# A two-layer graph network on one core: where the second softmax of a pair gets its exps, its store and its fetch

## The chip, the cores and the metric

The kernel runs on one core of a Trainium2 chip. The metric is the device time of one execution in microseconds (us). Before the change the median of three executions is 2647.58 us (2642.99 to 2649.26); the profiled execution has a span of 2647.7 us. All times below are of that profile, in us from the start of the span. The engines are TensorE (PE, its weight loads PEld), VectorE (DVE), ScalarE (ACT), GpSimd (POOL) and SyncE (SP), which issues nearly all transfers.

## What is computed

The input is x, 128 batches of 128 nodes by 512 features in float32, and adj, 128 batches of 128 by 128 flags. Layer 0 is masked attention with 8 heads of 64, layer 1 an attention over the same mask whose logits are sums of a node's two scalars. Both add their result to their input and normalise each row.

```python
# layer 0
q, k, v = x @ Wq + bq, x @ Wk + bk, x @ Wv + bv        # 8 heads of 64
logits  = einsum('bqhd,bkhd->bhqk', q, k) / 8
attn    = softmax(where(adj > 0, logits, -1e9), axis=-1)
x = layernorm(x + relu(einsum('bhqk,bkhd->bqhd', attn, v) @ Wo + bo))
# layer 1
Wh = x @ W
e  = leaky((Wh @ a1)[:, :, None] + (Wh @ a2)[:, None, :])
x  = layernorm(x + leaky(softmax(where(adj > 0, e, -9e15), axis=1) @ Wh))
```

## The kernel before

**Products.** All arithmetic is float32. Products with weights are done by Strassen's scheme with seven block products p1 to p7 (`ORDER`). Q, K and V are computed for a *group* of four batches at once (`group_product`, L367), the products of layer 0 with Wo and of layer 1 with W for a *pair* of batches (`pair_product`, L448). Each scheme is cut into seven steps: p1 with the read-out t0, p5, p6 with t2, p2 with c11, p7 with t3 and c22, p4 with c21, p3 with c12. The read-outs t0, t2, t3 are ScalarE copies (`st_t` at L344 or L348 for groups, `pr_t` at L459 for pairs), and p6, p7 and p4 add to the bank that they have just read, so TensorE can't go on with that bank until the copy is done. The results c11 to c12 are VectorE additions (L385, L693, L697, L772) or ScalarE copies. The group's banks are three of their own; all others (`psum`) share five in turn.

**Steps.** The main loop runs t from -3 to 123, one step for each batch; the last four batches follow by a written plan (`PLAN`). Every engine has its own queue, and the order in each is the order of the program (`manual_schedule`): there is no scheduler, and an instruction that waits holds all that follow on its engine. `group(n)` and `pair(n)` emit the next n pieces of the running group and pair products between the other work. In an even step t the pair product is layer 1's for batches t-6 and t-5, in an odd one layer 0's for t-3 and t-2. Each step also carries one batch of layer 1's attention (`Edge`, called `edge`, `fin` and `coming` in its three stages).

**Attention, around which the change is.** It goes by pairs of batches: `first` is the softmax of batch t, `sm` that of t+1, t even.
- `scores` (L520): TensorE forms the logits of both at the start of the even step, four banks.
- `maxima` = `add` (L534, mask onto the logits, VectorE) and `reduce` (L543).
- `exp` (L554) and `divide` (L568): one ScalarE instruction for each head, with `reciprocals` (L564, VectorE) between. An exp is followed by the read of its sum.
- `store` (L575) writes the weights to DRAM, `fetch` (L581) reads them back in four transfers with blocks of 32 moved, and `transpose` (L587, VectorE) turns the blocks: together the transposed weights.
- `attend` (L600): O^T = V^T times the transposed weights, eight products of 64 by 128 each way; `copy` (L614) reads it out with a bias on ScalarE, and `sum` forms the sums for the next product on GpSimd.

In an even step `first` does its exps, divisions, store and fetch, and at its end `sm` does exps 0 to 3 (L1183 to L1187). In the odd step `sm` does exps 4 to 7 among the pieces of layer 0, then its divisions, the last two after the fourth group piece (L1163); `sm.store` and `sm.fetch` stand behind all of that (L1170, L1176), and between the two stands the fetch of the edge's logits (`ez`, L1175). `sm.transpose` is the last VectorE piece before the two `attend` at the end of the odd step (L1193 to L1203). After `attend` come the scores of the next pair.

In the steps 0 to 3 there is not yet work of layer 1, and other branches of the loop give the order (L1030 to L1067).

Of the kernel before, what the change touches and what calls it, by code (L numbers as in the profile page):

```python
# [8 lines left out]
F32 = mybir.dt.float32  # L9
# [15 lines left out]
def kernel(  # L25
# [68 lines left out]
    big = ctx.enter_context(tc.tile_pool(name="big", bufs=2))  # L94
    work = ctx.enter_context(tc.tile_pool(name="work", bufs=1))
# [158 lines left out]
    def load_residual(b):  # L254

        X1[b] = work.tile([P, D], F32, name="x1", bufs=7)
        nc.sync.dma_start(X1[b], x[b])
# [610 lines left out]
    def on(b):  # L868
        return 0 <= b < B
# [14 lines left out]
    none = Nothing()  # L884
# [16 lines left out]
    first = sm = fin = edge = coming = none  # L901
# [77 lines left out]

    chores += right_blocks(places(wk)) + load_wv()  # L980
    END = B - GROUP
    for t in range(-3, END):
        pair_steps = []
        if t % GROUP == 1 and on(t + 3):
            rest = group_steps
            group_steps, v_pieces, fetch_v = products((t + 3) // GROUP)
            group_steps = rest + group_steps
        if t % 2 == 1 and on(t - 3):
            pair_steps = zero[(t - 3) // 2] = LayerZero((t - 3) // 2)
            pair_steps = pair_steps.steps()  # L990
        if t % 2 == 0 and on(t - 6):
            pair_steps = LayerOne((t - 6) // 2).steps()

        def group(n=1):
            for _ in range(min(n, len(group_steps))):
                group_steps.pop(0)()
            for _ in range(min((3 if t == -3 else 2 if t >= 0 else 1) * n, len(chores))):
                chores.pop(0)()

        def w1_chores(n):  # L1000
            for op in [w1_sums.pop(0) for _ in range(n)]:
                op()

        def pair(n=1):
            for _ in range(min(n, len(pair_steps))):
                pair_steps.pop(0)()

        if on(t + 2):
            load_mask(t + 2)
        if t == 0:  # L1010
            load_blocks(Wo, columns(wo), nc.sync, spread_rows=False)
            late_chores = right_blocks(places(wo)) + load_bias()
            w1_loads, w1_sums, w1_blocks = load_w1()
        if t == 1:
            chores += late_chores

        if t % 2 == 0:

            first, sm = (Softmax(t), Softmax(t + 1)) if on(t) else (none, none)
            first.scores()  # L1020
            sm.scores()
        coming.turn_blocks()
        if t % 2 == 1 and on(t - 3):
            zero[(t - 3) // 2].by()
            zero[(t - 3) // 2].bw()
        if later and t > 4:
            later.pop().go_back()
        if t == 5:
            group(2)
        if t < 3 and t % 2 == 0:  # L1030
            first.maxima()
            sm.add(0)
            sm.add(1)
            group(2)
            if on(t - 2):
                load_residual(t - 2)
            if t == 0 and on(GROUP):
                sum_x(1)()
            first.exp(0, 1, 2, 3)
            group()  # L1040
            first.reciprocals(0)
            first.exp(4, 5, 6, 7)
            first.reciprocals(1)
            sm.reduce()
            first.divide(0, 1, 2, 3)
            group()
            first.divide(4, 5, 6, 7)
            mask_float(t + 2)
        elif t < 3:
            group(2)  # L1050
            if on(t - 2):
                load_residual(t - 2)
            sm.exp(4, 5)
            group()
            sm.exp(6, 7)
            sm.reciprocals(0)
            sm.reciprocals(1)
            if t == 1:
                group()
            sm.divide(0, 1, 2, 3)  # L1060
            first.transpose()
            group()
            sm.divide(4, 5, 6, 7)
            if t == 1:
                group()
            if on(t + 2):
                mask_float(t + 2)  # L1067
        elif t == 4:

            layer = later.pop()  # L1070
            first.maxima()
            group()
            layer.apply(0)
            sm.add(0)
            sm.add(1)
            load_residual(2)
            if on(8):
                sum_x(2)()
            first.exp(0, 1)
            group()  # L1080
            first.exp(2, 3, 4, 5)
            sm.reduce()
            group()
            layer.store(1)
            layer.store(0)
            layer.fetch(1)
            layer.fetch(0)
            w1_chores(3)
            first.exp(6, 7)
            group()  # L1090
            first.reciprocals(0)
            first.reciprocals(1)
            first.divide(0, 1, 2, 3, 4, 5, 6, 7)
            mask_float(6)
        else:
            if t % 2 == 0:
                first.maxima()
            group()
            if t % 2 == 0:
                sm.add(0)  # L1100
                sm.add(1)
            if t == 3:
                w1_chores(3)
            if t == 5:
                turn_x1(4)
                x1_sums()
            edge = coming
            edge.add()
            fin.residual()
            if on(t - 2):  # L1110
                load_residual(t - 2)
            edge.maxima()
            fin.stats()
            fin.rstd()
            x1_sums()
            if t % GROUP == 0 and on(t + GROUP):
                sum_x(t // GROUP + 1)()
            pair()
            if t % 2 == 0:
                first.exp(0, 1, 2, 3)  # L1120
            else:
                sm.exp(4, 5)
            edge.exp()
            pair()
            if t % 2 == 0:
                first.exp(4, 5)
                sm.reduce()
            else:
                sm.exp(6, 7)
                first.transpose()  # L1130
            group()
            (first if t % 2 == 0 else sm).reciprocals(0)
            pair()
            if t % 2 == 0:
                first.exp(6)
            else:
                sm.reciprocals(1)
            fin.apply()
            fin.store()
            if t % 2 == 0:  # L1140
                first.exp(7)
            else:
                sm.divide(0, 1)
            edge.divide()
            pair()
            if t % 2 == 0:
                first.reciprocals(1)
                first.divide(0, 1, 2, 3)
            else:
                sm.divide(2, 3, 4, 5)  # L1150
            coming = Edge(t - 6) if on(t - 6) and t + 1 < END else none
            coming.sender()
            coming.store_sender()
            if t in (3, 5):
                w1_chores(2 if t == 3 else 4)
            if t == 5:
                for op in w1_blocks:
                    op()
            group()
            if t % 2 == 0:  # L1160
                first.divide(4, 5)
            else:
                sm.divide(6, 7)  # L1163
            pair()
            if t % 2 == 0:
                first.divide(6, 7)
            if on(t + 2):
                mask_float(t + 2)
            group()
        (first if t % 2 == 0 else sm).store()  # L1170
        if 0 <= t < 3:
            for load in w1_loads[4 * t : 4 * t + 4]:
                load()
        if t >= 6:
            coming.fetch_sender()  # L1175
        (first if t % 2 == 0 else sm).fetch()  # L1176
        for b in x_turns(t):
            transpose_x(b)
        for b in x_turns(t + 1):
            load_x(b)  # L1180
        if on(t + 2):
            mask(t + 2)
        if t % 2 == 0:  # L1183
            sm.exp(0, 1)
        pair(2)
        if t % 2 == 0:
            sm.exp(2, 3)  # L1187
        if t % 2 == 0 and on(t - 6):
            turn_x1(t)
        if t not in (0, 4):  # L1190
            group(21 if t % GROUP == 0 else 1)
        if t % 2 == 1:
            sm.transpose()  # L1193
        fin = edge
        fin.product()
        fin.copy()
        if t % 2 == 1:

            first.attend()
            sm.attend()  # L1200
            first.copy()
            sm.copy()
            sm.sum(0, 1, 2, 3)  # L1203

# [65 lines left out]
    for n in range(4):  # L1272
        jobs[f"s{n}"] = Softmax(END + n, homes[n])
    jobs["al"] = later.pop()
# [112 lines left out]
```

## Time and profile before

| | before |
|---|---|
| median of 3 executions | 2647.58 us |
| span of the profile | 2647.7 us |
| mean granted TensorE clock | 0.955 |
| TensorE without work | 207.7 us (span less busy 2440.0) |
| VectorE, ScalarE, GpSimd busy | 1810.6, 1515.2, 796.9 us |
| transfers | 395.31 MB, 149 GB/s; 48.4% of 16 engines in the main queue |
| four steps in the steady part (t = 7 to 123) | 81.2 us |
| store of 512 KB of weights, issue to landing (median) | 3.1 us |
| fetch of 128 KB of weights, issue to landing (median) | 2.8 us |

How to read it: the busy share of TensorE is an average and its ends are modelled, so the table says where there is time without work but not why. The waits of an engine, with the releaser beside each, say which work came last. The timeline then shows that work in order. The granted clock is a column of its own when the profile is cut into short windows: TensorE that is busy at a lower clock does less.

### The profile page before, as it was taken

The numbers are of one execution on the slowest core, as the hardware profiler recorded it, in microseconds if no ns is written. First come the engines' busy times: TensorE is split into PE (matmuls) and PEld (weight loads), VectorE is DVE, ScalarE is ACT, GpSimd is POOL, SyncE is SP. The second block draws the span as 40 slices with busy tenths as digits, with TensorE's granted clock in tenths as the row PEclk, the third lists the DMA queues.
The fourth block names the chain that finished last, engine by engine and source line by source line (L and its number), as shares of the span: only waits on it lengthen the run. The fifth ranks groups of instructions, "written<-read, shape, count | busy, mean of one in ns | idle before, by whom it ended". The sixth has DMA issues, their size and how long they took to land.

```text
span 2647.7 us, 44071 instructions
## 1 busy us (share of the span) xinstructions
PE 2440.0 (92%) x13362; PEld 2069.0 (78%) x13362; DVE 1810.6 (68%) x3718; ACT 1515.2 (57%) x5459; POOL 796.9 (30%) x1191
## 2 busy tenths in 40 slices
PE   8789999999999999999999999999999999999997
PEld 7678778778787787787877877878778778778775
DVE  5557666766767676667667676766666767766668
ACT  3546556555565565555655655655556555555575
POOL 1222332322323233323223232332222333322325
PEclk9899999999999999999999999999999999999999
DMA  7444454454445445444454444444444544454443
GB/s 203 131 144 147 148 156 146 147 154 146 148 143 157 150 142 155 151 151 148 149 158 151 142 152 150 143 153 149 149 147 142 161 151 148 149 156 149 141 151 117
DMA packets 435564, 395.31 MB, mean 149 GB/s; under 512 B 108280, under 2 KB 339328, under 8 KB 435328
## 3 DMA queue, kind: packets, MB, share of 16 engines
q1 hardware_dynamic: 435008, 392.23, 48.4%
q8 instruction: 107, 1.75, 0.3%
q14 instruction: 129, 1.06, 0.1%
q10 hardware_dynamic: 320, 0.26, 0.0%
HBM read 248.58 MB, written 143.72 MB: 148 GB/s over the span
## 4 chain that ended last, share of the span: by engine, by line
PE 59%; DMA 15%; DVE 10%; ACT 7%; SPq 5%; issue 3%; POOL 1%; DVEq 0%; POOLq 0%; ACTq 0%
PE st_y L367 16%; PE st_w L367 10%; PE p_y L448 10%; PE lg L520 7%; DMA pa_dram<-pa 7%; DMA paz<-pa_dram 6%; PE p_w L448 5%; DVE pa L587 4%; ACT pa L568 4%; PE st_x L367 4%; SPq L581 4%; PE p_oT L600 3%; PE p_x L448 3%; PE p_h L841 2%; DMA xz<-in_x_dram 1%
## 5 line engine op out<-in xcount | busy, mean ns | idle before, releaser
L650 POOL TENSOR_SCALAR ve<-mv 128x1 f32<-128x1 f32 x256 | 70.2, 274 | 1415.5 <-DVE mv L646 1410.0
L554 ACT ACTIVATE pa<-pa,nmax 128x128 f32<-128x128 f32 x1008 | 394.1, 395 | 3.4 <-DVE nmax L543 3.4
L568 ACT ACTIVATE pa<-pa,rs 128x128 f32<-128x128 f32 x1008 | 327.2, 393 | 26.5 <-DVE rs L564 26.2
L600 PE MATMUL p_oT<-pa,v 128*64 128x128 f32 x2016 | 160.2, 309 | 177.3 <-DVE pa L587 176.9
L600 PEld LDWEIGHTS p_oT<-pa,v 128*64 128x64 f32 x2016 | 124.4, 152 | 238.5 <-DVE pa L587 191.8
L534 DVE TENSOR_TENSOR pa<-lg,mf 128x512 f32<-128x512 f32 x252 | 161.7, 683 | 170.2 <-PE lg L520 170.2
L614 ACT ACTIVATE oT<-p_oT,b_cols 128x128 f32<-128x128 f32 x504 | 143.7, 368 | 223.5 <-PE p_oT L600 222.4
L459 ACT COPY pr_t<-p_y 128x257 f32<-128x257 f32 (+1 forms) x375 | 138.1, 368 | 203.3 <-PE p_y L448 201.2
L344 ACT COPY st_t<-st_y 128x512 f32<-128x512 f32 x192 | 110.3, 574 | 192.8 <-PE st_y L367 192.5
L587 DVE STREAM_TRANSPOSE pa<-paz 128x1024 f32<-128x1024 f32 x126 | 156.7, 1244 | 80.3 <-DMA paz<-pa_dram 79.3
L520 PE MATMUL lg<-kT,qT 64*128 64x128 f32 x2048 | 204.9, 377 | 0.0
L520 PEld LDWEIGHTS lg<-kT,qT 64*128 64x128 f32 x2048 | 189.7, 282 | 17.5 <-issue 17.1
L554 ACT ACTIVATION_READ_ACCUMULATOR pa<-pa,nmax 128x1 f32 x1008 | 193.5, 192 | 0.0
L652 POOL TENSOR_TENSOR rstd<-ve,mhalf 128x1 f32<-128x1 f32 x256 | 176.4, 689 | 21.3
L348 ACT ACTIVATE st_t<-st_y,b_cols 128x256 f32<-128x256 f32 x192 | 80.4, 469 | 159.7 <-PE st_y L367 159.6
L543 DVE TENSOR_REDUCE nmax<-pa 128x8 f32<-128x1024 f32 x126 | 151.7, 1204 | 2.3
L276 POOL TENSOR_TENSOR oS<-oT 128x256 f32<-128x256 f32 x63 | 45.7, 725 | 314.0 <-ACT oT L614 314.0
L448 PE MATMUL p_y<-wo,oT 128*128 128x256 f32 x504 | 129.9, 380 | 4.5 <-ACT p_y L469 3.1
L448 PE MATMUL p_y<-wo,oS 128*128 128x256 f32 x504 | 129.5, 379 | 0.5 <-ACT pr_t L459 0.5
L448 PE MATMUL p_y<-w,x1T 128*128 128x257 f32 x496 | 128.3, 381 | 1.8 <-ACT wk L459 1.8
L448 PE MATMUL p_y<-w,x1S 128*128 128x257 f32 x496 | 128.0, 380 | 0.2 <-ACT wk L459 0.2
L367 PE MATMUL st_y<-xT,wk 128*128 128x256 f32 x512 | 126.3, 390 | 0.0
(201 smaller groups left out, 5920.5 us busy)
## 6 DMA issues: line engine op xcount, KB each, us to landing
pa_dram<-pa SPq DMA_DIRECT2D x126, 512.0 KB, 3.1
paz<-pa_dram SPq DMA_DIRECT2D x504, 128.0 KB, 2.8
wv_n<-wv SPq DMA_DIRECT2D x224, 256.0 KB, 2.7
x<-in_x_dram SPq DMA_DIRECT2D x128, 256.0 KB, 2.9
x_dram<-x SPq DMA_DIRECT2D x128, 256.0 KB, 2.1
xz<-x_dram SPq DMA_DIRECT2D x512, 64.0 KB, 2.0
xz<-in_x_dram SPq DMA_DIRECT2D x496, 64.0 KB, 2.3
out_dram<-z SPq DMA_DIRECT2D x120, 256.0 KB, 2.0
```

Of the source, the lines that this page charges most:

```text
L367: nc.tensor.matmul(p[:, m, :], lhs, rhs, start=start and m == 0 and kc == 0, stop=True, skip_group_check=True,)
L448: nc.tensor.matmul(p[:, :width], xs()[n][:, kc, :], w[:, PLACE[n], kc, :], start=start and kc == 0, stop=True, skip_group_check=True,)
L459: nc.scalar.copy(t[:, :width], p[:, :width])
L520: nc.tensor.matmul(self.lg[r][:, c, :], q[rows, c, cols], k[rows, c, cols], start=c == 0, stop=True, skip_group_check=True,)
L534: nc.vector.tensor_add(by_head[:, r * NC : (r + 1) * NC], self.lg[r].rearrange("p c (b k) -> p c b k", b=4), mf.unsqueeze(1).to_broadcast( ...
L543: nc.vector.tensor_reduce(self.nmax, by_head, AX.XY, ALU.max, negate=True)
L554: nc.scalar.activation(self.pa[:, :, h, :], self.pa[:, :, h, :], AF.Exp, bias=self.nmax[:, h : h + 1], accum_out=self.sums[:, h : h + 1],)
L568: nc.scalar.activation(self.pa[:, :, h, :], self.pa[:, :, h, :], AF.Copy, scale=self.rs[:, h : h + 1])
L587: nc.vector.transpose(self.paT.rearrange("p h (a i) -> p a h i", i=32), self.paz.rearrange("p a (h k) -> p a h k", k=32),)
L600: nc.tensor.matmul(self.oT[r * HD : (r + 1) * HD, c, :], v[:, h * HD : (h + 1) * HD], self.paT[:, r * NC + c, :], start=c == 0, stop=True, ...
L614: nc.scalar.activation(OT[pair][:, c, h * P : (h + 1) * P], self.oT[:, c, :], AF.Identity, bias=b_cols[:, 1, c : c + 1],)
L652: nc.gpsimd.tensor_tensor(self.r, ve, mhalf, ALU.pow)
```

## The change

It reorders the second softmax of each pair (`sm`) and moves the first O^T of the kernel.

- Its exps: 0 to 5 at the end of the even step (three before and three after the next-to-last pair piece), 6 and 7 at the start of the odd step, ahead of the odd step's first pieces.
- Its reciprocals in the odd step come right after the edge's residual, ahead of the edge's maxima; its divisions are drawn together to the third pair piece, with `sm.store` right behind them. Before, the store stood at the end of the step.
- Its fetch comes ahead of the fetch of the edge's logits, and its transpose ahead of the last piece of the pair product (p3 with c12 of layer 0, and what follows it on VectorE), which it stood behind.
- The O^T of batches 0 and 1, which ended step 1, is held until the end of step 2, and `sm.transpose` of batch 1 goes into step 2. As their weights live longer, batches 2 and 3 get their weights' tile in buffers of other tags (`x1T` and `v`), through the `homes` argument that `Softmax` has already.

The aim is that the transposed weights of `sm` are there when TensorE reaches its O^T. The core of the diff ("..." where lines are left out):

```diff
+    first_homes = {
+        2: {"pa": lambda shape: work.tile(shape, F32, name="pa", tag="x1T")},
+        3: {"pa": lambda shape: big.tile(shape, F32, name="pa", tag="v", bufs=3)},
+    }
...
+        if t % 2 == 1:
+            sm.exp(6, 7)
         if t == 5:
             group(2)
...
             first.divide(0, 1, 2, 3)
+            if t == 2:
+                held[1].transpose()
...
-            sm.exp(4, 5)
             group()
-            sm.exp(6, 7)
             sm.reciprocals(0)
...
             fin.residual()
             if on(t - 2):
                 load_residual(t - 2)
+            if t % 2 == 1:
+                sm.reciprocals(0)
+                sm.reciprocals(1)
             edge.maxima()
...
             else:
-                sm.divide(2, 3, 4, 5)
+                pair()
+                sm.divide(0, 1)
+                edge.exp()
+                sm.divide(2)
+                pair()
+                sm.divide(3, 4, 5)
+                first.transpose()
+                group()
+                pair()
+                fin.apply()
+                fin.store()
+                sm.divide(6, 7)
+                sm.store()
+                edge.divide()
+                pair()
...
-        (first if t % 2 == 0 else sm).store()
+        if t % 2 == 0:
+            first.store()
+        elif t < 3:
+            sm.store()
...
+        if t % 2 == 1:
+            sm.fetch()
         if t >= 6:
             coming.fetch_sender()
-        (first if t % 2 == 0 else sm).fetch()
+        if t % 2 == 0:
+            first.fetch()
...
         if t % 2 == 0:
-            sm.exp(0, 1)
-        pair(2)
+            sm.exp(0, 1, 2)
+        pair()
+        if t % 2 == 1 and t != 1:
+            sm.transpose()
+        pair()
         if t % 2 == 0:
-            sm.exp(2, 3)
+            sm.exp(3, 4, 5)
...
-        if t % 2 == 1:
-            sm.transpose()
         fin = edge
         fin.product()
         fin.copy()
-        if t % 2 == 1:
-
-            first.attend()
-            sm.attend()
-            first.copy()
-            sm.copy()
-            sm.sum(0, 1, 2, 3)
+        if t == 1:
+            held = first, sm
+        elif t == 2 or t % 2 == 1:
+
+            both = held if t == 2 else (first, sm)
+            for softmax in both:
+                softmax.attend()
+            for softmax in both:
+                softmax.copy()
+            both[1].sum(0, 1, 2, 3)
```

More of the change, by code (lines that the diff above doesn't have):

```diff
@@ L1017 @@
         if t % 2 == 0:
-            first, sm = (Softmax(t), Softmax(t + 1)) if on(t) else (none, none)
+            first, sm = none, none
+            if on(t):
+                first, sm = (Softmax(b, first_homes.get(b)) for b in (t, t + 1))
             first.scores()
@@ L1117 @@
                 sum_x(t // GROUP + 1)()
-            pair()
             if t % 2 == 0:
+                pair()
                 first.exp(0, 1, 2, 3)
[L1121 to L1125, printed above, removed]
+                edge.exp()
+                pair()
                 first.exp(4, 5)
                 sm.reduce()
[L1128 to L1134, printed above, removed]
-                first.exp(6)
[L1136 to L1140, printed above, removed]
-                first.exp(7)
[L1142 to L1146, printed above, removed]
+                group()
+                first.reciprocals(0)
+                pair()
+                first.exp(6)
+                fin.apply()
+                fin.store()
+                first.exp(7)
+                edge.divide()
+                pair()
                 first.reciprocals(1)
@@ L1149 @@
             else:
-                sm.divide(2, 3, 4, 5)
+                pair()
+                sm.divide(0, 1)
+                edge.exp()
+                sm.divide(2)
+                pair()
+                sm.divide(3, 4, 5)
+                first.transpose()
+                group()
+                pair()
+                fin.apply()
+                fin.store()
+                sm.divide(6, 7)
+                sm.store()
+                edge.divide()
+                pair()
             coming = Edge(t - 6) if on(t - 6) and t + 1 < END else none
@@ L1161 @@
                 first.divide(4, 5)
-            else:
-                sm.divide(6, 7)
             pair()
@@ L1183 @@
         if t % 2 == 0:
-            sm.exp(0, 1)
-        pair(2)
+            sm.exp(0, 1, 2)
+        pair()
+        if t % 2 == 1 and t != 1:
+            sm.transpose()
+        pair()
         if t % 2 == 0:
-            sm.exp(2, 3)
+            sm.exp(3, 4, 5)
         if t % 2 == 0 and on(t - 6):
```

## Prediction

> **What bounds the kernel now.** I read the page's first two parts, then the waits of TensorE, then the timeline around the longest of them, then the granted clock in short windows. TensorE is busy 92% of the span and the chain that ended last is mostly its own work:
>
> ```profile
> PE 2440.0 (92%) x13362; PEld 2069.0 (78%) x13362; DVE 1810.6 (68%) x3718; ACT 1515.2 (57%) x5459; POOL 796.9 (30%) x1191
> ...
> PE 59%; DMA 15%; DVE 10%; ACT 7%; SPq 5%; issue 3%; POOL 1%; DVEq 0%; POOLq 0%; ACTq 0%
> ```
>
> One wait makes up nearly all the rest (columns: us in total, times, longest). It comes once in each pair of steps:
>
> ```profile
> PE p_oT L600 <- DVE pa L587: 176.9, 62, 7.1
> PE p_h L841 <- DVE wk L836: 4.3, 4, 2.6
> ```
>
> It is the O^T of the second batch of a pair (`sm.attend`), which waits for the block transpose of its weights, which waits for a store and a fetch through DRAM. The timeline of one pair (start, duration) shows the chain and what follows it:
>
> ```profile
> 1035.88 0.32 SPq L575 DMA_DIRECT2D pa_dram<-pa  x1
> ...
> 1038.84 2.23 SPq L581 DMA_DIRECT2D paz<-pa_dram  x4
> ...
> 1043.86 1.25 DVE L587 STREAM_TRANSPOSE pa<-paz 128x1024 f32<-128x1024 f32 x1 [0.56 <-DMA paz<-pa_dram]
> ...
> 1045.16 1.51 PE L600 MATMUL p_oT<-pa,v 128*64 128x128 f32 x16 [2.83 <-DVE pa L587]
> ...
> 1046.60 3.24 PE L520 MATMUL lg<-kT,qT 64*128 64x128 f32 x32
> ```
>
> The clock granted to TensorE (the number after the five busy times) is full before the gap and falls after it:
>
> ```profile
> 1036.00:1040.00 4.00, 4.00 (x20) 3.54 (x19) 3.78 (x8) 0.32 (x2) 0.00 (x0) 1.00 0.46 152
> 1040.00:1044.00 4.00, 2.33 (x21) 1.28 (x19) 3.31 (x9) 2.56 (x7) 2.25 (x4) 1.00 0.71 197
> 1044.00:1048.00 4.00, 2.84 (x28) 2.51 (x30) 1.73 (x3) 1.14 (x4) 0.08 (x1) 0.71 0.54 172
> ```
>
> So the gap is paid twice: 2.83 us of idleness, and then scores that take 3.24 us. In a pair where the clock happened to stay up, the same scores take 2.06:
>
> ```profile
> 1166.77 1.09 PE L600 MATMUL p_oT<-pa,v 128*64 128x128 f32 x16 [3.25 <-DVE pa L587]
> 1167.80 2.06 PE L520 MATMUL lg<-kT,qT 64*128 64x128 f32 x32
> ```
>
> **What the Trainium skill says.** "TensorE: Matmul & The Clock Gate", Part 1 (the HAM clock gate), describes two clock states, full and half, with a fall after an idle window of about 3.4 us and a return after about as long of work. The trace agrees on the half and on the length (half-clock from 1045.8 to 1049), but gaps of 2.17 us already bring it on in most pairs; gaps of 1.90, 1.66 and 1.42 us elsewhere in this trace left the clock full. "DMA: Bandwidth & Descriptors", Rules for kernel authors, says a DMA that reads what an earlier one wrote must wait for that one's completion; the trace agrees, the fetch starts 2.96 us after the store. "PSUM — Partial Sum Buffer", Engine vs sequencer instructions, says ScalarE and VectorE queues are strictly first in, first out; the trace agrees, the last two divisions of the second batch stand behind a bias copy that waits for TensorE (below).
>
> **What a group of four steps costs.** Call pair A the steps t%4 = 0, 1 and pair B t%4 = 2, 3. From the second O^T of a pair to that of the next, less the wait, A takes 37.1 us at full clock (1166.77 to 1206.09, less 2.18). B takes 37.0 with slow scores (1045.16 to 1085.55, less 3.38); it has one group product fewer (10 against 11, 1.73 us each), so 35.4 at full clock, and a slow clock costs 1.6. Four steps of full-clock work: 72.5. From the second O^T of t=7 (189.23) to that of t=123 (2544.31) are 29 such groups, 81.2 us each: 72.5, about 5.6 of waits (A 2.4, B 3.2) and 3.1 of slow clock.
>
> **The change part by part.** It adds and removes no instruction of compute; TensorE's order is the same after t=2. All effects are waits.
>
> *Exps.* The second batch's exps 4 and 5 go to the end of the even step, 6 and 7 to the start of the odd one. Two exps are 0.77 us (start to start 0.385). At the end of the even step ScalarE is idle 1.06 us before `v<-st_y` and 2.00 before `z<-p_h`: hidden, cost nothing. In the odd step exps 6 and 7 stand ahead of the bias copy, `e_turned` and `pr_t`; `pr_t` comes about 0.15 us later and its reader on TensorE (p6 at 1030.79) keeps over 1 us: nothing.
>
> *Division and store, pair A.* Before, six divisions ran at 1032.12 and the last two only at 1035.17, behind the bias copy of a group product that ended on TensorE at 1034.44. Now all eight are due before it: reciprocals at about 1028, four exps and divisions follow, the last two come after `pr_t` of p6 (readable at 1031.85), so at 32.2 to 32.8. Store at 1032.85 for 1035.88, 3.0 us sooner. In pair B, ScalarE: divisions from 1069.55, `st_t` at 71.75, `pr_t` 72.2, last two 72.5 to 73.1. But the output store stands ahead on the DMA queue and waits for VectorE, which now does the transpose and the kT addition first: about 1073.7. Store at about 1074.05 for 1075.96, 1.9 sooner.
>
> *Fetch and transpose.* Store to landing is 2.90 us in the A sample and 3.97 in B, where a weight load lay just ahead; I take 2.9 and 3.3. Fetch to landing is 4.9 and 4.1. Transpose and semaphore 1.3. A: 1032.85+2.9+4.9+1.3 = 1042.0, while the first batch's O^T ends at 1042.1: no wait left. B: 1074.05+3.3+4.1+1.3 = 1082.75 against 1081.95: 0.8 left (0.3 to 1.8 with landings of 2.9 to 3.97 and the store a little off). Both are below the 1.9 that left the clock full: no slow scores. The fetch of `ez` goes behind that of `paz`: 1.8 us later, and its reader comes after the transpose: nothing.
>
> *The wait that moves.* `sm.transpose` now stands ahead of the last block of LayerZero on VectorE. Behind it queue y, residual, statistics, two `apply`, an addition and `e_turned`: 3.2 to 3.8 us from the end of the transpose (0.39+0.69+0.69+0.18+0.51+0.27+0.51, gaps, and 0.68 in A). The first to wait for these is the bank of the next scores, which y frees: transpose end +0.45, scores at +0.87: nothing. Then the additions of the mask to the scores start at 3.7 us after the second O^T instead of 2.2. In the full-clock sample everything after them on VectorE is without a break until c11 of LayerOne, and its slack is small:
>
> ```profile
> 1179.46 0.40 ACT L798 ACTIVATE e<-mf,wh 128x128 f32<-128x128 bf16 x1 [0.90 <-DVE wh L772]
> ...
> 1180.35 0.35 ACT L459 COPY pr_t<-p_y 128x257 f32<-128x257 f32 x1
> ```
>
> TensorE adds p4 to that bank at 1181.14, 0.44 us after. So 1.5 us later costs TensorE about 1.0 in A's even step. For B, a pair with the additions at +3.8 (1209.91) has `pr_t` at +14.7 where full-clock TensorE is due at +14.4: 0.25. The unknown is how much VectorE slips: 0 to 1.8 us for A and B together.
>
> *Start.* First O^T moved behind t=2's products: the wait of 7.07 us goes, and one slow start. t=2's scores start at 65.3 instead of 75.34. But the eight copies of O^T (2.3 us) and two more exps lie ahead of the LayerZero bias on ScalarE: p_y at about 81.6 instead of 91.90, a new wait of some 2 us. Gain 10; then 3 at t=3 (3.48 before) and 3 for each of the next two pairs: 19. The two `pa` tiles in other buffers add no wait: x1T is first written at t=5, and the v buffers at t=4.
>
> *Sum.* 72.5 + 0 + 0.8 + 1.0 + 0.25 + 0.25 for jitter of the transfers = 74.8 a group; 6.4 us less, times 29 = 186; with the start 205; 2647.6 - 205 = about 2443 us.
>
> **Rivals.** (1) VectorE catches up and nothing new waits: 73.1 a group, 81.2-73.1 = 8.1, times 29 = 235, and 19: 2394. For it: DVE 68% busy. Against it: the unbroken row after the scores. (2) The clock keeps falling, or stalls at p4 and a late fetch eat more: 3 us a group more than forecast, 2530. For it: 2.17 us was enough for the slow clock; a stall and a late store in B could come near it. Against: 1.90 did not. (3) Slower: the store leaves no sooner since ScalarE or the output store ahead of it holds it, while VectorE, which now waits for the fetch with LayerZero's last block behind it, hands its 3.7 us on to the next scores: 1.5 us more a pair for 62 pairs, less 10 for the start: 2647.6 + 83 = 2731. Against it: the last two divisions lose the very wait that held them.
>
> **How the numbers follow.** Forecast 0.62, rival 1 0.14, rival 2 0.2, rival 3 0.04. Time 2443; range 2398 to 2525, from just above rival 1 to nearly rival 2. Faster 0.95, same 0.01, slower 0.04.
>
> **What would show it.** The wait of p_oT on L587 falls from 176.9 to some 30 us; the mean clock rises from 0.955 to 0.98 or more and the scores take 2.06 us in most pairs; the store follows p6's `pr_t` in A; new waits of TensorE for `pr_t` (L459) appear, more in A. Wrong would be: scores still at 3.2 to 3.8, or a wait on VectorE where the scores' bank is freed.

## The result, and the profile after

The changed kernel takes 2459.68 us (median of 4 runs, 2457.11 to 2464.29), against 2645.28 us (4 runs, 2635.23 to 2649.26) for the kernel before in the same comparison. The ratio is 0.9306, 95% interval 0.9275 to 0.9336: about 186 us less. The forecast was 2443.

The page's busy times and the chain of work that ended last, by engine, after the change:

```profile
PE 2355.6 (96%) x13362; PEld 1972.3 (80%) x13362; DVE 1836.2 (75%) x3718; ACT 1517.7 (62%) x5459; POOL 770.5 (31%) x1191
...
PE 45%; DVE 25%; DMA 11%; ACT 9%; SPq 4%; issue 4%; POOL 1%; DVEq 0%; POOLq 0%; ACTq 0%
```

The profiled span fell from 2647.7 to 2457.2 us, and TensorE is busy for 96% of it instead of 92%. Its own busy time fell too, by 84.4 us, with the same 13362 matmuls: the same work ran at a higher clock (mean granted clock 0.997, before 0.955). The chain has moved a step: DMA's share went from 15% to 11%, and VectorE's from 10% to 25%. VectorE comes up again below.

The waits of TensorE after the change (us in total, times, longest):

```profile
PE p_y L448 <- ACT pr_t L459: 36.6, 44, 1.2
PE p_oT L600 <- DVE pa L587: 32.9, 34, 3.1
PE p_h L841 <- DVE wk L836: 5.0, 5, 2.6
```

The wait of O^T for the transpose has gone from 176.9 us to 32.9, and from 62 occurrences to 34. A wait that was not among those shown of before now leads the list: a product of layer 1 (`LayerOne` in the kernel, as `LayerZero` is layer 0) that waits for ScalarE's read-out copy `pr_t`.

The timeline (start, duration) of a pair B, then, after the "...", of the pair A that follows it:

```profile
1061.30 0.34 SPq L865 DMA_DIRECT2D out_dram<-z  x1
1061.74 0.38 SPq L575 DMA_DIRECT2D pa_dram<-pa  x1
...
1064.61 3.16 SPq L581 DMA_DIRECT2D paz<-pa_dram  x4
...
1071.52 1.09 PE L600 MATMUL p_oT<-pa,v 128*64 128x128 f32 x16 [1.66 <-DVE pa L587]
...
1072.54 2.06 PE L520 MATMUL lg<-kT,qT 64*128 64x128 f32 x32
...
1100.63 0.33 SPq L575 DMA_DIRECT2D pa_dram<-pa  x1
...
1103.31 1.75 SPq L581 DMA_DIRECT2D paz<-pa_dram  x4
...
1108.11 1.25 DVE L587 STREAM_TRANSPOSE pa<-paz 128x1024 f32<-128x1024 f32 x1
...
1109.03 1.97 PE L600 MATMUL p_oT<-pa,v 128*64 128x128 f32 x32
1110.92 2.06 PE L520 MATMUL lg<-kT,qT 64*128 64x128 f32 x32
```

In pair A both O^T now run in one go (`x32`, no bracket): the transpose starts with the first matmuls of the output product before them and is done under the first O^T. In pair B a wait of 1.66 us is left, and the scores behind it still take 2.06 us, so the clock stays up. The clock in the three 4 us windows around pair A's O^T (five busy times, then the granted clock, the DMA share and GB/s) says the same:

```profile
1104.00:1108.00 4.00, 4.00 (x20) 3.54 (x19) 3.50 (x8) 0.00 (x0) 0.00 (x0) 1.00 0.57 148
1108.00:1112.00 4.00, 4.00 (x54) 3.04 (x54) 3.87 (x8) 3.20 (x11) 1.29 (x4) 1.00 0.24 70
1112.00:1116.00 4.00, 4.00 (x32) 3.53 (x30) 3.97 (x7) 1.42 (x5) 3.41 (x5) 1.00 0.51 173
```

TensorE is busy for 12.00 us of the 12. In the groups of instructions the 2048 matmuls of the scores fell from 204.9 us to 132.1.

**Where the 190.5 us of the span came from.** I cut both traces at the second O^T of t=7 and of t=123, 29 groups of four steps apart, as the forecast did (189.23 and 2544.31 before; 169.62 and 2352.30 after), and read TensorE's busy time and waits in between:

| us a group of four steps | before | after | forecast of after |
|---|---|---|---|
| TensorE busy | 75.72 | 73.01 | 72.5 |
| O^T waits for the transpose | 5.49 | 1.02 | 0.8 and 0.25 of jitter |
| products wait for `pr_t` | 0 | 1.23 | 1.0 and 0.25 |
| total | 81.21 | 75.26 | 74.8 |

The steady part gave 5.95 us 29 times, 172.4 us: 129.8 from the wait of O^T and 78.6 from the shorter busy time, that is from the clock, less 35.6 of the new wait and 0.4 of gaps too short for the list of waits. The start up to t=7 gave 19.6 us, and the end took back 1.5.

### The profile page after: what moved, and what is told of

It is laid out like the page before. It is cut to its first block, busy times and chain, and to the rows that moved or that the text cites. A ratio compares the mean times of both kernels' runs of the same rounds, so it can differ in the third digit from the quotient of the medians.

```text
span 2457.2 us, 44158 instructions
## 1 busy us (share of the span) xinstructions
PE 2355.6 (96%) x13362; PEld 1972.3 (80%) x13362; DVE 1836.2 (75%) x3718; ACT 1517.7 (62%) x5459; POOL 770.5 (31%) x1191
## 3 DMA queue, kind: packets, MB, share of 16 engines
q8 instruction: 107, 1.75, 0.3%
## 4 chain that ended last, share of the span: by engine, by line
PE 45%; DVE 25%; DMA 11%; ACT 9%; SPq 4%; issue 4%; POOL 1%; DVEq 0%; POOLq 0%; ACTq 0%
PE st_y L367 14%; PE p_y L448 9%; PE st_w L367 7%; DMA pa_dram<-pa 5%; PE p_w L448 5%; DVE pa L534 4%; ACT pa L568 4%; PE st_x L367 3%; PE p_h L841 3%; SPq L581 3%; DMA ez<-e_dram 3%; DMA paz<-pa_dram 2%; DVE pa L587 2%; DVE nmax L543 2%; DVE z L665 2%
## 5 line engine op out<-in xcount | busy, mean ns | idle before, releaser
L568 ACT ACTIVATE pa<-pa,rs 128x128 f32<-128x128 f32 x1008 | 334.1, 396 | 33.9 <-DVE rs L564 33.9
L600 PEld LDWEIGHTS p_oT<-pa,v 128*64 128x64 f32 x2016 | 108.0, 136 | 89.0 <-DVE pa L587 41.7
L448 PE MATMUL p_y<-w,x1T 128*128 128x257 f32 x496 | 134.3, 393 | 37.2 <-ACT pr_t L459 35.6
L600 PE MATMUL p_oT<-pa,v 128*64 128x128 f32 x2016 | 132.6, 278 | 33.5 <-DVE pa L587 32.9
L652 POOL TENSOR_TENSOR rstd<-ve,mhalf 128x1 f32<-128x1 f32 x256 | 146.5, 572 | 21.3
L448 PEld LDWEIGHTS p_y<-w,x1T 128*128 128x128 f32 x496 | 89.4, 190 | 70.8 <-ACT pr_t L459 58.5
L520 PE MATMUL lg<-kT,qT 64*128 64x128 f32 x2048 | 132.1, 279 | 0.0
L520 PEld LDWEIGHTS lg<-kT,qT 64*128 64x128 f32 x2048 | 119.4, 188 | 12.3 <-issue 11.9
L367 PE MATMUL st_y<-wv_n,xT 128*128 128x256 f32 x512 | 122.4, 382 | 2.6 <-ACT st_t L344 2.6
```

The costliest lines, as they stand in the source:

```text
L367: nc.tensor.matmul(p[:, m, :], lhs, rhs, start=start and m == 0 and kc == 0, stop=True, skip_group_check=True,)
L448: nc.tensor.matmul(p[:, :width], xs()[n][:, kc, :], w[:, PLACE[n], kc, :], start=start and kc == 0, stop=True, skip_group_check=True,)
L520: nc.tensor.matmul(self.lg[r][:, c, :], q[rows, c, cols], k[rows, c, cols], start=c == 0, stop=True, skip_group_check=True,)
L568: nc.scalar.activation(self.pa[:, :, h, :], self.pa[:, :, h, :], AF.Copy, scale=self.rs[:, h : h + 1])
L600: nc.tensor.matmul(self.oT[r * HD : (r + 1) * HD, c, :], v[:, h * HD : (h + 1) * HD], self.paT[:, r * NC + c, :], start=c == 0, stop=True, ...
L652: nc.gpsimd.tensor_tensor(self.r, ve, mhalf, ALU.pow)
```

## The experiments

What I held after the result: the early store takes the gap before the second O^T away, with it the slow clock, and hands a smaller stall on to LayerOne through VectorE. Against it stood that the gain might come from the start, from the order of the fetches or from the exps, and that the stall might come from ScalarE. For each kernel the table gives the profiled span, the sum of all rows of TensorE's waits, TensorE's busy time, and the mean of one matmul of the scores (ns), which tells how often they ran slowly. The changed kernel was timed in the first comparison only, and the kernel before read 2641.3 to 2645.3 us in the four; so a difference to the changed kernel of some 4 us says nothing.

| kernel | median us | span | waits | busy | scores, ns |
|---|---|---|---|---|---|
| before | 2645.28 | 2647.7 | 199.5 | 2440.0 | 377 |
| after | 2459.68 | 2457.2 | 93.2 | 2355.6 | 279 |
| filler in the gap | 2555.44 | 2551.5 | 78.2 | 2465.0 | 283 |
| before + later first O^T | 2631.17 | 2630.0 | 192.1 | 2429.6 | 369 |
| after, first O^T back | 2469.65 | 2467.1 | 97.6 | 2360.0 | 282 |
| after, exps back | 2475.28 | 2472.7 | 102.6 | 2361.3 | 283 |
| after, `ez` fetched first | 2591.74 | 2592.9 | 172.4 | 2411.5 | 336 |
| before, `paz` fetched first | 2630.56 | 2622.8 | 194.1 | 2420.1 | 364 |
| after, B's transpose last | 2422.57 | 2420.3 | 63.2 | 2348.8 | 284 |
| after, both transposes last | 2500.32 | 2501.6 | 126.7 | 2366.9 | 308 |
| after, sender later | 2446.9 | 2446.1 | 87.1 | 2350.0 | 279 |
| after, store before z | 2444.25 | 2442.0 | 78.5 | 2354.3 | 280 |
| last three single edits together | 2409.05 | 2413.0 | 60.9 | 2342.8 | 282 |

### What the clock alone is worth: work put into the gap

```diff
-        def attend(self):
+        def attend(self, filler=0):
...
+            for _ in range(filler):
+                nc.tensor.transpose(self.oT[:, 3, :], ident, ident)
             for c in range(NC):
...
             first.attend()
-            sm.attend()
+            sm.attend(16)
```

> The kernel before with 16 transposes of the identity on TensorE between the two O^T of each pair, into the bank that the second O^T overwrites; they take about 1.8 us of the 2.2 to 3.8 us of the wait and no result uses them. Account A (an idle gap is paid twice, once as a wait and once as scores at half clock, 1.6 us in nine pairs of ten): the wait itself ends no sooner but the scores take 2.06 us, so 80 to 95 us less than before: about 2555. Account B (the scores are slow for another reason, such as the banks or the loads of weights): no change or slower by what the transposes take, 2645 or more.

Measured: 2555.44 us (2553.33 to 2555.67), ratio to before 0.9672 [0.9653, 0.9692], clock 0.995. The timeline of one pair, TensorE:

```profile
1159.70 1.97 PE L598 MATMUL p_oT<-ident 128*128 128x128 f32 x16
1161.94 1.09 PE L602 MATMUL p_oT<-pa,v 128*64 128x128 f32 x16 [0.28 <-DVE pa L587]
1162.97 2.06 PE L520 MATMUL lg<-kT,qT 64*128 64x128 f32 x32
```

The second O^T starts when the transpose lets it, as before. Only now TensorE is not idle until then, and the scores take 2.06 us. This kernel does 1.97 us more work a pair and is 88 us faster (2643.6, the kernel before beside it, less 2555.44): the slow clock after the gaps alone cost about 88 us, 1.4 us a pair in the mean of 62. That is the term which the forecast put at 3.1 us a group (90 us). "TensorE: Matmul & The Clock Gate", Part 1, of the Trainium skill puts the penalty of warming up at under 1% of a typical span, and describes besides (HAM oscillation) a kernel that pays it again with every tile. This case is of the second kind: the slow clock came back with most pairs and cost 3.3%.

**Which gaps bring the slow clock.** Not the length of the gap alone: before the change, one of 3.48 us left the clock full and one of 2.17 us did not. In all 13 traces the granted clock falls only on a beat of 3.413 us, to within 1 ns (the first 30 us left aside). Cut on that beat, the two gaps of the kernel before (they end at 514.92 and 638.06) look like this (window, its length, TensorE busy, granted clock, DMA share and GB/s):

```profile
509.80:513.22 3.41, 1.64 (x18) 1.00 0.84 243
513.22:516.63 3.41, 1.71 (x28) 1.00 0.37 118
516.63:520.04 3.41, 3.41 (x36) 1.00 0.54 165
...
636.10:639.51 3.41, 1.45 (x22) 1.00 0.44 144
639.51:642.92 3.41, 3.41 (x31) 0.50 0.61 187
```

The longer gap is shared by two beats, with 1.77 and 1.70 us of idleness; the shorter one puts 1.96 us into a single beat, and the next runs at half the clock. I counted all 9160 beats at full clock of the 13 traces: none of the 8886 with less than 1.74 us of idleness was followed by half the clock, each of the 200 with 2.0 us or more was, and of the 74 in between 52 were. (The idleness is that of the recorded matmuls, whose ends are modelled.)

### The start

The edit of the first kernel puts the first O^T of the changed kernel back into step 1; the second makes that edit alone in the kernel before.

```diff
         fin.copy()
-        if t == 1:
-            held = first, sm
-        elif t == 2 or t % 2 == 1:
+        if t % 2 == 1:
...
-            both = held if t == 2 else (first, sm)
-            for softmax in both:
-                softmax.attend()
...
+            first.attend()
+            sm.attend()
```

> The changed kernel with the first O^T left at the end of step 1 (no held pair, no tiles in other buffers), all else as changed. My account: only the start loses, so about 10 to 13 us more than the changed kernel's 2460: 2470 to 2475, and every scores product after t=4 still takes 2.06 us. Rival (the move of the first O^T shifts the phase of everything after it and carries a large part of the gain): 2520 or more.

> The kernel before with only the first O^T moved to the end of step 2, none of the changes in the steady steps. My account: 10 to 14 us under the kernel before (2645), so about 2633, with the wait of O^T for the transpose still about 2.8 us a pair. Rival (the start carries the gain): 2580 or less.

Measured: put back, 2469.65 us (2468.39 to 2472.47), ratio 0.9352 [0.9329, 0.9375], so 10.0 us over the changed kernel. Alone, 2631.17 (2620.10 to 2642.48, 18 runs), ratio 0.9953 [0.9939, 0.9967], 12.4 us under the kernel before beside it. With it back, the longest wait of O^T is 7.0 us again. The forecast's figure for this edit was 10. It adds to the rest, since it has its own gap, but it is only some 6% of the gain.

### The exps

```diff
         if t % 2 == 1:
-            sm.exp(6, 7)
+            sm.exp(4, 5, 6, 7)
...
-            sm.exp(0, 1, 2)
+            sm.exp(0, 1)
...
-            sm.exp(3, 4, 5)
+            sm.exp(2, 3)
```

> The changed kernel with exps 4 and 5 of the second batch back in the odd step (0 to 3 at the end of the even step, 4 to 7 at the start of the odd one), store and fetch as changed. Account A (the place of the divisions and of the store carries the gain, two exps are 0.77 us that pair A can hide and pair B not wholly): 10 to 25 us more than 2460. Account B (having the exps out of the way of the odd step carries the gain): most of it goes, 2550 or more.

Measured: 2475.28 us (2474.61 to 2477.89), ratio 0.9373 [0.9353, 0.9392]: 15.6 us over the changed kernel. Over some 29 pairs of each kind, pair A's store leaves 0.60 us later and its transpose starts about 0.55 us later (medians, counted from the output product `p_h`). In pair B nothing moves: the store goes out 6.07 us ahead of `p_h` in both kernels, behind the output store that stands ahead of it. So it is pair A's store that the exps move. The waits of O^T account for 8.5 of the 15.6 us (32.9 to 41.4 in all) and busy time for 5.7; why busy time rose I didn't follow.

### The order of the two fetches

The diff puts the fetch of `paz` ahead of that of `ez`, and the forecast wrote beside it only that `ez` loses nothing. The first kernel turns the order back in the changed kernel, the second makes the new order alone in the kernel before.

```diff
-        if t % 2 == 1:
-            sm.fetch()
         if t >= 6:
             coming.fetch_sender()
+        if t % 2 == 1:
+            sm.fetch()
```

> The changed kernel with the fetch of the edge's logits (ez) ahead of the fetch of the second batch's weights again, as before the change. The fetch of ez takes 1.8 us of the queue and waits for its own store. If the place of the fetch matters: pair B's fetch leaves about 1.5 us later and O^T there waits about 2.5 us, pair A's wait becomes 0 to 1 us, and some scores are slow again: 50 to 90 us more than 2460. If it is hidden: within 5 us of 2460.

> The kernel before with only the fetch of the second batch's weights ahead of the fetch of ez in odd steps; exps, divisions, store, transpose and start as before. Account A (the order of the two fetches counts only when the store is early: before, the ez fetch ended at 1038.43 and the store landed at 1038.78): no change, 2636 to 2648. Account B (the order alone carries the 132 us that it cost to undo it): about 2515.

Measured: turned back, 2591.74 us (2588.10 to 2594.69), ratio 0.9809 [0.9782, 0.9835]: 132 us over the changed kernel, more than either account allowed. Alone, 2630.56 (2624.62 to 2631.28), ratio 0.9957 [0.9941, 0.9974]: 11 us less, far from what it is worth in the changed kernel, and 5 us below the range expected. The wait of O^T is nearly as before (172.1 us for 176.9); what fell is the number of slow scores (364 ns in the mean for 377). That the gaps happened to fall otherwise on the clock's beat would do it; this is not shown. The timeline of a pair with `ez` first (DMA queue, VectorE, TensorE):

```profile
997.84 0.41 SPq L806 DMA_DIRECT2D e_dram<-e  x1
1000.86 2.94 SPq L812 DMA_DIRECT2D ez<-e_dram  x4
1003.89 1.80 SPq L581 DMA_DIRECT2D paz<-pa_dram  x4
...
1008.70 1.25 DVE L587 STREAM_TRANSPOSE pa<-paz 128x1024 f32<-128x1024 f32 x1 [3.83 <-DMA paz<-pa_dram]
...
1010.00 1.98 PE L600 MATMUL p_oT<-pa,v 128*64 128x128 f32 x16 [3.09 <-DVE pa L587]
```

and the row of the DMA queue's own waits that belongs to it:

```profile
SPq L812 <- DMA e_dram<-e: 95.5, 60, 2.5
```

The queue issues one transfer after the other, and a fetch must wait for the landing of what it reads (as "DMA: Bandwidth & Descriptors", Rules for kernel authors, of the Trainium skill has it). With the weights stored early, `e_dram` is stored after them; the fetch of `ez` then waits for the landing of that store, once in 60 pairs, and takes its 1.8 us or more of issuing, and the fetch of `paz`, whose data are long there, stands behind both. From store to fetch it is now 4.73 us in pair A and 5.58 in pair B, for 2.71 and 2.93 in the changed kernel, and the transpose starts 1.94 and 2.04 us later. In the kernel before the same order cost nearly nothing: there the store of `e` was out 1.58 us before that of the weights (1034.30 and 1035.88 in the pair shown), and `ez` was issued (1036.30 to 1038.43) while the weights' store was still landing. So the early store and the order of the fetches are worth much only together. Of the span's 136 us, 79 are waits and 56 busy time, and the scores are back at 336 ns.

### The stall handed on: transpose, sender

If VectorE's lateness behind the transpose is the cause, the transpose put behind the last block of LayerZero in pair B should take the stall of the next even step away. If `e` in front of `pr_t` on ScalarE is the cause, moving the sender should.

```diff
-        if t % 2 == 1 and t != 1:
+        if t % 4 == 1 and t != 1:
             sm.transpose()
...
             group(21 if t % GROUP == 0 else 1)
+        if t % 4 == 3:
+            sm.transpose()
```

> The changed kernel with the second batch's transpose back at the end of the odd step in pair B only (t%4 = 3), behind the last block of layer 0. Account A (TensorE's wait of 1.2 us for pr_t in pair A's even step comes from VectorE, which is held by the transpose of the pair B before it and is late with everything behind it): that wait falls from 36 us to under 10, 25 to 35 us less than 2460. Account B (the wait for pr_t comes from ScalarE's own load, eight exps and six divisions ahead of it): within 5 us of 2460.

Measured: 2422.57 us (2421.33 to 2426.46), ratio 0.9175 [0.9154, 0.9197]: 37 us under the changed kernel. Waits of TensorE:

```profile
PE p_oT L600 <- DVE pa L587: 40.1, 35, 3.3
...
PE p_y L448 <- ACT pr_t L459: 2.7, 13, 0.5
```

The wait for `pr_t` has gone from 36.6 to 2.7, while that of O^T rose by 7.2 only: pair B's fetch lands so late that LayerZero's last block fits in ahead of it. The transpose starts at the same place (1.76 us after `p_h`, 1.80 in the changed kernel). The block that VectorE used to do after it is now done before.

The same move in both pairs:

```diff
         pair()
-        if t % 2 == 1 and t != 1:
-            sm.transpose()
         pair()
...
             group(21 if t % GROUP == 0 else 1)
+        if t % 2 == 1 and t != 1:
+            sm.transpose()
```

> The changed kernel with the transpose last on VectorE in both pairs, as before the change. In pair A the weights land when VectorE has just done the statistics; y, residual, statistics, apply and an addition (3.1 us) then stand ahead of the transpose, O^T waits about 2.7 us and many scores are slow again; pair B is as with the transpose last in B alone. Account A (VectorE's order in A sets when O^T starts): 100 to 120 us more than 2423. Account B (the landing of the fetch sets it, and VectorE's order there costs nothing): within 10 us of 2423.

Measured: 2500.32 us (2496.98 to 2503.46), ratio 0.9463 [0.9449, 0.9477]: 78 us over the kernel with the move in pair B alone, where more was expected. In pair A the data are there in time, so the transpose starts 2.9 us later for nothing and O^T waits again (104.0 us in all, 62 times). But only part of the scores ran slowly (308 ns in the mean). Of the 28 gaps of 2.17 to 2.18 us in this trace 14 brought the half clock and 14 did not, while all 17 of that length in the kernel before did: the length is the same, the place on the beat is not. The early transpose of the change is right in pair A and wrong in pair B.

```diff
             coming = Edge(t - 6) if on(t - 6) and t + 1 < END else none
-            coming.sender()
-            coming.store_sender()
+            if t % 2 == 1:
+                coming.sender()
+                coming.store_sender()
...
             if t % 2 == 0:
+                coming.sender()
+                coming.store_sender()
                 first.divide(6, 7)
```

> The changed kernel with the edge's sender logits (e, L798) and their store behind pr_t of p7 in the even step, instead of ahead of two divisions and that pr_t. Account A (the wait for pr_t goes through e, which waits for VectorE's c11): the wait of TensorE for pr_t goes, 30 to 36 us less than 2460. Account B (pr_t is late because ScalarE is behind with its own work): about 12 us less at most, one instruction of 0.4 us in 29 steps.

Measured: 2446.90 us (2444.78 to 2449.28), ratio 0.9265 [0.9244, 0.9286]: 13 us less, and the wait for `pr_t` still 28.2 us. One stall with the sender out of the way (ScalarE and TensorE):

```profile
781.21 0.69 ACT L568 ACTIVATE pa<-pa,rs 128x128 f32<-128x128 f32 x2 [0.98 <-DVE rs L564]
781.81 0.35 ACT L459 COPY pr_t<-p_y 128x257 f32<-128x257 f32 x1
...
782.21 1.14 PE L448 MATMUL p_y<-w,x1T 128*128 128x257 f32 x4 [0.95 <-ACT pr_t L459]
```

Now two divisions ahead of `pr_t` wait 0.98 us for the reciprocals, which VectorE hands over late as well. ScalarE is where the lateness passes through, by `e` or by the reciprocals; VectorE is where it comes from, as the kernel with B's transpose last shows.

### Pair B's store

```diff
                 pair()
-                fin.apply()
-                fin.store()
                 sm.divide(6, 7)
                 sm.store()
+                fin.apply()
+                fin.store()
                 edge.divide()
```

> The changed kernel with the last two divisions and the store of the second batch's weights ahead of the edge's normalisation and its output store in the odd step. If the output store ahead in the queue holds the weights' store in pair B: the store leaves 0.6 to 1.0 us sooner there, the wait of O^T falls from 33 us to about 8, 20 to 28 us less than 2460. If the landing of the fetch sets the wait (four issues that took 3.2 us in pair B): under 10 us less.

Measured: 2444.25 us (2443.45 to 2448.09), ratio 0.9258 [0.9236, 0.9279]: 15 us less, between the two accounts. Pair B's store leaves 0.88 us sooner, so it was the output store that held it, but the transpose starts only 0.63 us sooner: from fetch to transpose it is 5.02 us, for 4.52. The wait of O^T falls from 32.9 to 18.0 and that for `pr_t` stays at 35.7. Why the earlier fetch takes longer to land I didn't settle.

### The three together

The edits of "B's transpose last", "sender later" and "store before z" in one kernel.

> The changed kernel with three further moves together: the transpose last in pair B only, the weights' store ahead of the output store, the sender logits behind pr_t. If each of them works on a wait of its own: the transpose gave 37 us, the store 15; the sender gave 13, but of a wait that the transpose already takes away: 2460 - 37 - 15 - 0 to 5 = 2403 to 2408. If they work on the same wait: about 2420, no better than the transpose alone.

Measured: 2409.05 us (2405.53 to 2414.76), ratio to before 0.9120 [0.9105, 0.9136], just above the first of the two ranges expected. It beats both kernels, the changed one by 51 us. Its page and its waits of TensorE:

```profile
PE 2342.8 (97%) x13362; PEld 1982.2 (82%) x13362; DVE 1822.7 (76%) x3718; ACT 1509.2 (63%) x5459; POOL 783.5 (32%) x1191
```

```profile
PE p_oT L600 <- DVE pa L587: 38.0, 33, 2.5
```

No row for `pr_t` is left among the first ones. Alone the three edits gave 37, 13 and 15 us, 65 in sum, and together 51. The sender and the transpose work on the same wait, that for `pr_t`. The account behind the expected sum fails for the store too: the wait of O^T is 38.0 us, for 40.1 with B's transpose last alone and 18.0 with the store first alone. So the earlier store no longer shortens that wait, and the sum came out nearly right by luck. The reason is in the trace: in 22 of 30 pairs B of the steady part the transpose begins without a break behind VectorE's other work, and the median transpose begins 0.58 us after the last landing of its data, for 0.12 in the changed kernel. What sets the wait that is left there is mostly VectorE and no longer the fetch. Where the 13.5 us below the kernel with B's transpose last come from is not shown in full: the profiled executions, 2413.0 and 2420.3, differ by 7.3 us only, 6.0 of it busy time. The group of four steps takes 73.7 us, with 72.5 of TensorE's work in it.

## Why the prediction was right, and where it was off

The forecast came true, with a time inside its range and 17 us above the figure given. Step by step:

- *The gap is paid twice, and both halves go.* Shown. The waits of O^T fell by 144 us, and the filler kernel, which leaves the gap's length and takes only its idleness away, prices the clock at 88 us where the forecast had 90. In the changed kernel's steady part the clock gave 78.6.
- *Waits below 1.9 us leave the clock full.* In the steady part it came out so: all scores of the main loop took 2.06 us, and the longest wait of O^T there was 1.66 us. As a rule it does not hold. In this very trace a gap of 1.89 us near 51 us was followed by half the clock, and with the three edits one of 1.75 us was (at 688.7); what counts is the idleness within one beat. The forecast had its 1.9 from a single gap, and it was luck that the waits stayed well below.
- *Pair A's store at 1032.85.* Times in the two traces are matched by the `p_h` just ahead of the odd step (1024.75 before, 1092.54 after, 67.79 later): 1100.64 expected, 1100.63 measured. Median gain 3.05 us, forecast 3.0. Landing and fetch took 2.7 and 4.8, for 2.9 and 4.9. No wait left: right.
- *Pair B's store at 1074.05.* Matched in the same way (12.30 earlier): 1061.75 expected, 1061.74 measured, behind the output store as the forecast had it. Median gain 1.91, forecast 1.9. The wait of O^T was put at 0.8 and 0.25 for jitter, and is 1.02 a group.
- *The exps cost nothing.* Right, and they earn some 15 us. Pair B's store would leave as early without them.
- *The wait that moves.* Right in place and nearly in size: 1.23 us a group for `pr_t`, forecast 1.25. In the timeline after, A's even step:

```profile
1074.62 0.94 DVE L665 TENSOR_SCALAR x<-x,mv,rstd 128x512 f32<-128x512 f32 x1 [0.53 <-POOL rstd L652]
1075.48 1.28 DVE L534 TENSOR_TENSOR pa<-lg,mf 128x512 f32<-128x512 f32 x2
...
1086.84 0.35 ACT L459 COPY pr_t<-p_y 128x257 f32<-128x257 f32 x1
1087.24 1.14 PE L448 MATMUL p_y<-w,x1T 128*128 128x257 f32 x4 [1.17 <-ACT pr_t L459]
```

  The additions start 3.96 us after the second O^T (1071.52), forecast 3.7. The rest is a wait of 0.53 us for GpSimd's `rstd` and an apply of 0.94 us for 0.51, which the forecast did not have. The stall is 1.17 us for 1.0, and pair B's is smaller than its 0.25 (0.14 in the one read).
- *The route of that stall* was half right. The forecast followed it from c11 through `e` to `pr_t`. Moving `e` gave 13 us of some 37, and the reciprocals took its place; moving the transpose gave all 37. The chain of work had pointed there: VectorE's share rose from 10% to 25%.
- *The fetch of `ez` behind that of `paz`: "nothing".* This is what the forecast left out, although it did not move the sum. As a cost it was nothing, but the forecast's "store to landing, then the fetch" silently assumed it. Without it the same early store gives 132 us less. The order of work on the DMA queue belonged among the causes, not among the edits that cost nothing.
- *The start.* 19 us up to t=7; measured 19.6. The edit itself was put at 10 and gave 10 and 12. The new wait of the product for the LayerZero bias is 2.04 us at 82.38, forecast some 2 at 81.6.

The term that was mis-sized is the full-clock work: 72.5 us a group, measured 73.01, 0.5 us 29 times or 15 of the 17 us. The 72.5 is not wrong as such: the kernel with all three edits does a group in 72.5 us of busy time. A part of the excess is shown: the products that wait for `pr_t` (`p_y<-w,x1T`) take 393 ns in the mean, for 383 with all three edits, 4.9 us in all; the four behind a stall take 1.14 us, as in the lines above. So the new wait has a small second price, at full clock. Where the other 10 us lie I did not find; it stays open.

The rivals: VectorE does not catch up (rival 1; its 73.1 a group does not follow from the terms given, which without the two waits for `pr_t` make 73.55), and the clock does not keep falling (rival 2), though two single edits (fetches in the old order, both transposes last) bring rival 2's picture about. Rival 3's VectorE, with LayerZero's last block queued behind the transpose, is real, but it cost 36 us and did not turn the gain into a loss.

## What to carry to other kernels

Price an idle gap of TensorE with what runs behind it: here 2.8 us of waiting took 1.4 us more from the scores, in the mean, and unused work of TensorE in the gap alone made the kernel 3.3% faster, before anything was done about its cause. When a round trip through memory is moved up, follow every instruction that stands in the same issue queue between its store and its fetch, for a neighbour that waits for a later store can take most of the gain, here 132 of 186 us. And an early place in an in-order queue is worth it only where the data are there: the same early transpose was needed in one pair and cost 37 us in the other. Gains of single edits don't add up where one edit changes what another waits for: the store first gave 15 us alone, and no shorter wait of O^T behind the late transpose.

## What the runs showed of the hardware that I had not expected

- A queue of transfers is issued in order across its waits, and issuing itself takes time: four fetches of 128 KB take 1.75 to 1.80 us when nothing holds them. A fetch whose data had landed left 2.0 to 2.65 us later (medians of pairs A and B) behind one that waited for its own store: 132 us in 2592.
- The clock granted to TensorE falls to half on a beat of 3.413 us, after a beat with about 1.75 to 2.0 us of idleness in it or more. So a gap of 3.48 us that lies across two beats cost only itself, and one of 2.17 us, 1.96 of it within one beat, cost a beat at half the clock besides. It comes back on the beat, too: of the 284 beats at half the clock, the 239 followed by full clock had at most 0.46 us of idleness, and the 45 followed by another at half had 0.45 us or more.
- In the changed kernel it takes 2.7 us (pair A) and 2.9 us (pair B) in the median from the issue of the 512 KB store to that of its fetch, and 4.8 and 4.5 us more until the transpose starts. Where pair B's store left 0.88 us sooner, the second part grew from 4.52 to 5.02; why stays open.
- VectorE's scaled copies ran at two speeds: `z` (L665) and `att` (L836) took 1.38 and 1.11 us in the even step of a pair A (from 1082.98 in the trace after), beside GpSimd's additions for `xS`, and 0.52 and 0.29 in that of a pair B (from 1045.22), with GpSimd idle. Over the whole trace the 30 `z` that met an idle GpSimd took 0.52 to 0.54 us, the other 87 from 0.50 to 1.39. No run here took GpSimd's work away, so that it is the cause is argued, not shown.
